# Product with edge_w: three of seven products of each column group split again into seven of half size, their operand sums on GpSimd, the stage written in a fixed order

## The chip, the cores and the metric

The kernel runs on one core of a Trainium2 chip. The metric is the device time of one execution in microseconds. Before the change it is 1904.14 us, the median of three runs (1903.38 to 1904.72). In this text TensorE is PE in the profile, VectorE is DVE, ScalarE is ACT, GpSimd is POOL and SyncE, which issues most loads, is SP.

## The reference, cut to what matters

Inputs are x (4096 x 512), adj (4096 x 4096, about 1.6% of it positive, the rest zero), and the weights of two graph layers. Everything is float32.

```python
x = layernorm(x + relu(adj @ (max(sign(x), 0) @ sign(w0).T)))     # layer 0
node_att = softmax(x @ node_w, axis=0)                            # layer 1, on the new x
h = x @ edge_w                                                    # 4096 x 512: the stage of the change
e = where(adj > 0, h @ h.T, -9e15)
out = adj * (node_att * softmax(e, axis=1)) @ (x @ w1)
x = layernorm(x + out + bias)
```

## The kernel before, in words

**Stages.** The core computes layer 0 row block by row block (up to 505 us), then h (505 to 602 us), then the products h @ h.T with their masked exponentials (602 to about 1000 us), and then the aggregation. This change is in the second stage, and in how it meets the first and the third.

**The product with edge_w.** The new x lies transposed in SBUF as x1T, four slabs of 128 features by 4096 nodes. Wanted is h transposed, hT, of the same shape. The 4096 nodes are eight column chunks of 512; chunk g and chunk g + 4 form column group g (g = 0 to 3). edge_w is cut into 2 x 2 blocks of 256 x 256, and x1T of one group into 2 x 2 blocks of 256 x 512. The function seven (L90) multiplies these 2 x 2 blocks with seven products instead of eight, in the manner of Strassen and Winograd. The seven left operands (left_h) are l11, l12, s4, l22, s1, s2, s3, with four sums made once per kernel by GpSimd (L480 to L483). The right operands are r11, r21, r22, t4, t1, t2, t3, with four differences (t1 to t4) per group made by VectorE in rights_h (L498 to L504) one group ahead. A product is number m = 0 to 6: left operand m times right operand m. It has two halves q (128 rows of output each, one PSUM bank each), and each half takes two matmuls of 128 x 128 by 128 x 512. So a group is 28 matmuls 512 columns wide. A float32 matmul shows as two weight loads and two matmul instructions in the trace.

**Sums of products.** Six PSUM banks (three pairs) hold the running sums. When a product ends, ScalarE copies a bank to hT (L113, L127), or VectorE adds a bank to a block of hT (L116, L122, L123, L131, L135): ten additions of 128 x 512 and four copies per group. c11, c12, c21, c22 are the four blocks of hT of the group; c21 and c22 are the lower feature half, c12 and c22 the chunk g + 4. Tiles of PSUM and SBUF come from pools with a fixed number of buffers, and a new tile waits until an earlier one is no longer read. Accesses of different engines to one PSUM bank are put in sequence, also where they touch different columns.

**What runs beside it.** After each half of a product, between_h is called. It steps the last row block's leftovers from layer 0 (late: eight small VectorE sums, L394 to L397, and DMA issues from GpSimd, L399 and L400), the next group's differences, and premask (L331 on). premask turns pieces of adj (128 x 1024) into bf16 masks: SyncE loads a piece into a buffer (L345, 512 KB), VectorE turns it into a mask in place (L339), GpSimd issues the store to DRAM (L340, 256 KB), and the buffer is loaded again. 26 of 80 pieces are left for this stage. Seven buffers go round (pieces of the tiles more, single, ends and sums_l), and a piece is masked when only three buffers are free, so a load has several calls of time to land. The next stage reads the masks back.

**Order.** Tile's scheduler sets the order of the instructions on each engine in this stage, from dependencies and its own estimate of times; VectorE and ScalarE (not TensorE) are in a written order in the stage before. The last row block of layer 0 ends inside this stage: its normalisation (L356 to L363) on VectorE and its transposes (L419) on TensorE. The next stage begins with operand sums for its own products on VectorE (L783 to L796, L874 to L877, L892 to L895, L908 to L921), which need the finished hT and memory that this stage gives up.

Of the kernel before, what the change touches and what calls it, by code (L numbers as in the profile page):

```python
# [11 lines left out]
F32 = mybir.dt.float32  # L12
# [17 lines left out]
def kernel(  # L30
# [59 lines left out]
    def seven(lop, rop, dests, after):  # L90

# [6 lines left out]
        def multiply(bank, m, first, then):  # L98
            for q in range(2):
                for k in range(K):  # L100
                    nc.tensor.matmul(  # L101
                        banks[bank][q],
                        lop(m, q)[k],
                        rop(m)[k],
                        start=(first and k == 0),
                        stop=(k == K - 1),
                        skip_group_check=not first,
                    )
                then(banks[bank][q], q, *dests[q])
                after(None, None)  # L110

        def m1(ps, q, c11, c12, c21, c22):
            nc.scalar.copy(c21, ps)  # L113

        def u2(ps, q, c11, c12, c21, c22):
            nc.vector.tensor_add(c12, c21, ps)  # L116
# [28 lines left out]

# [13 lines left out]
    with (  # L159
# [270 lines left out]
        with tc.manual_schedule(engines={mybir.EngineType.DVE, mybir.EngineType.Activation}):  # L430
            for n in range(NB):
# [62 lines left out]
        def rights_h(g):  # L494
# [1459 lines left out]
```

## Time and profile before

| | |
|---|---|
| median of three runs | 1904.14 us |
| profiled execution, its own time | 1903.96 us |
| its span | 1902.2 us |
| TensorE busy, of the span | 1890.8 us (99%) |
| VectorE, ScalarE, GpSimd busy | 1527.5, 1024.6, 314.1 us |
| product with edge_w, first to last matmul | 505.2 to 602.1 us |
| matmul instructions of L101 | 224 (two per matmul) |

A line of a timeline reads: start, duration, engine, line of the kernel, operation, output <- inputs, shapes, and how many instructions are merged. In the table of stages each engine has its busy time and the number of its instructions, then the granted TensorE clock, the share of the DMA engines that was busy, and GB/s. "Landing" is the time from the issue of a DMA to its completion.

### The profile page before, as it was taken

The numbers are of one execution on the slowest core, as the hardware profiler recorded it, in microseconds if no ns is written. First come the engines' busy times: TensorE is split into PE (matmuls) and PEld (weight loads), VectorE is DVE, ScalarE is ACT, GpSimd is POOL, SyncE is SP. The second block draws the span as 40 slices with busy tenths as digits, with TensorE's granted clock in tenths as the row PEclk, the third lists the DMA queues.
The fourth block names the chain that finished last, engine by engine and source line by source line (L and its number), as shares of the span: only waits on it lengthen the run. The fifth ranks groups of instructions, "written<-read, shape, count | busy, mean of one in ns | idle before, by whom it ended". The sixth has DMA issues, their size and how long they took to land.

```text
span 1902.2 us, 21262 instructions
## 1 busy us (share of the span) xinstructions
PE 1890.8 (99%) x7054; PEld 1263.4 (66%) x7054; DVE 1527.5 (80%) x2421; ACT 1024.6 (54%) x1669; POOL 314.1 (17%) x449
## 2 busy tenths in 40 slices
PE   9999999999999999999999999999999999999998
PEld 6888888888645656565667556666666666656646
DVE  7777677776877689888896887898879988898947
ACT  6433333333211567666777666665676567667732
POOL 0133132232331111111110111111111101110100
PEclk9999999999999999999999999999999999999999
DMA  9889898898585379577795978878777878787831
GB/s 321 299 322 362 308 339 323 330 353 321 179 295 190 141 267 346 191 259 277 286 334 166 327 279 297 287 288 300 273 278 287 294 270 277 268 318 253 286 114 56
DMA packets 143919, 521.00 MB, mean 274 GB/s; under 512 B 15040, under 2 KB 15040, under 8 KB 136128
## 3 DMA queue, kind: packets, MB, share of 16 engines
q1 hardware_dynamic: 64368, 235.43, 36.7%
q0 software_dynamic: 67632, 248.54, 34.2%
q10 hardware_dynamic: 11808, 35.66, 5.0%
q8 instruction: 56, 0.92, 0.2%
q14 instruction: 55, 0.45, 0.1%
HBM read 397.93 MB, written 121.63 MB: 273 GB/s over the span
## 4 chain that ended last, share of the span: by engine, by line
PE 89%; DVE 7%; ACT 2%; DMA 1%; issue 1%; ACTq 0%; SPq 0%; DVEq 0%
PE bank L1413 33%; PE acc L460 11%; PE acc L459 11%; PE bank L1011 11%; PE seven L101 5%; PE po L1563 4%; PE pt L707 3%; PE bank L806 2%; PE bank L970 2%; PE bank L933 2%; PE bank L745 2%; DVE lent L1182 1%; PE pt L419 1%; DVE slot L1182 1%; PE acc L253 1%
## 5 line engine op out<-in xcount | busy, mean ns | idle before, releaser
L1413 PE MATMUL bank<-lent,lop 128*128 128x256 f32 (+1 forms) x1368 | 433.0, 466 | 1.1 <-DVE lent L1194 0.7
L459 PE MATMUL acc<-xw,hi 128*128 128x512 f32 x960 | 376.4, 392 | 0.0
L460 PE MATMUL acc<-xw,lo 128*128 128x512 f32 x960 | 374.2, 390 | 0.0
L1413 PEld LDWEIGHTS bank<-lent,lop 128*128 128x128 f32 x1368 | 259.3, 190 | 146.1 <-issue 119.9
L1413 PE MATMUL bank<-slot,lop 128*128 128x512 f32 (+1 forms) x928 | 335.4, 508 | 0.4 <-DMA lop<-lop_d 0.2
L1413 PEld LDWEIGHTS bank<-slot,lop 128*128 128x128 f32 x928 | 176.0, 190 | 136.8 <-issue 121.3
L449 ACT CAST hi<-at 128x1024 fp32r<-128x1024 f32 x120 | 126.5, 1054 | 203.2 <-PE acc L459 152.9
L1424 ACT COPY over<-bank 128x512 f32<-128x512 f32 x200 | 116.0, 585 | 198.1 <-PE bank L1413 194.5
L460 PEld LDWEIGHTS acc<-xw,lo 128*128 128x128 f32 x960 | 180.3, 188 | 37.1 <-DVE lo L451 0.3
L459 PEld LDWEIGHTS acc<-xw,hi 128*128 128x128 f32 x960 | 180.3, 188 | 36.8
L451 DVE TENSOR_TENSOR lo<-at,hi 128x1024 fp32r<-128x1024 f32 x120 | 147.8, 1232 | 64.6 <-ACT hi L449 64.1
L678 ACT ACTIVATE line<-line,nmax_c 128x512 f32<-128x512 f32 x160 | 115.2, 726 | 22.4 <-DVE nmax_c L669 22.0
L669 DVE CUSTOM_DVE_ANT_0 line<-lent,slot 128x512 f32<-128x512 bf16 x144 | 93.1, 687 | 9.5 <-ACT slot L708 6.8
L1575 DVE SCALAR_TENSOR_TENSOR xb<-po,f,xb 128x256 f32<-128x256 f32 x84 | 40.3, 481 | 75.0 <-PE po L1563 70.8
L1386 ACT COPY bank<-over 128x512 f32<-128x512 f32 x144 | 86.8, 603 | 0.0
L707 PEld LDWEIGHTS pt<-ident,lent 128*128 128x128 f32 x406 | 50.9, 141 | 36.6 <-issue 24.2
L745 PE MATMUL bank<-hT 128*128 128x512 f32 (+3 forms) x256 | 75.1, 433 | 0.0
L1182 DVE CUSTOM_DVE_ANT_1 lent<-lent,line 128x2048 f32<-128x2048 f32 x32 | 73.0, 2283 | 1.1 <-DMA lent<-s_d 1.1
L708 ACT COPY slot<-pt 128x512 f32<-128x512 f32 (+3 forms) x125 | 68.0, 554 | 10.8 <-PE pt L707 10.8
L420 ACT COPY x1T<-pt 128x512 f32<-128x512 f32 x32 | 18.8, 587 | 101.7 <-PE pt L419 101.7
L1188 ACT ACTIVATE slot<-slot 128x2048 f32<-128x2048 f32 x35 | 67.3, 1924 | 10.8 <-DMA slot<-in_adj_t_dram 10.8
L1182 DVE CUSTOM_DVE_ANT_1 slot<-slot,line 128x2048 f32<-128x2048 f32 x32 | 73.1, 2284 | 0.0
(356 smaller groups left out, 3280.1 us busy)
## 6 DMA issues: line engine op xcount, KB each, us to landing
lop<-lop_d SPq DMA_DIRECT2D x154, 512.0 KB, 4.4
at<-in_adj_t_dram SPq DMA_DIRECT2D x60, 1024.0 KB, 7.3
slot<-in_adj_t_dram POOLq DMA_DIRECT2D x37, 1024.0 KB, 8.1
s_d<-slot POOLq DMA_DIRECT2D x32, 1024.0 KB, 7.6
slot<-s_d POOLq DMA_DIRECT2D x31, 1024.0 KB, 7.4
lent<-s_d POOLq DMA_DIRECT2D x29, 1024.0 KB, 8.2
lent<-in_adj_t_dram POOLq DMA_DIRECT2D x27, 1024.0 KB, 7.6
lent<-in_adj_dram SPq DMA_DIRECT2D x48, 512.0 KB, 6.2
```

Source lines behind the costliest of these rows:

```text
L101: nc.tensor.matmul(banks[bank][q], lop(m, q)[k], rop(m)[k], start=(first and k == 0), stop=(k == K - 1), skip_group_check=not first,)
L449: nc.scalar.copy(hi, aq)
L451: nc.vector.tensor_sub(lo, aq, hi.bitcast(F32))
L459: nc.tensor.matmul(acc, hi[:, c, :], xw[:, kb, :], start=(kb == 0), stop=False)
L460: nc.tensor.matmul(acc, lo[:, c, :], xw[:, kb, :], start=False, stop=(kb == NB - 1))
L678: nc.scalar.activation(line, line, AF.Exp, bias=nmax_c[:, b, c : c + 1], scale=-1.0, accum_out=sum_c[:, b, c : c + 1])
L707: nc.tensor.transpose(pt[:, j, :], src[:, ts(j, P)], ident)
L745: nc.tensor.matmul(pe[:, lo * P :], hT[:, k, ts(A * BG + i, P)], hT[:, k, (B * BG + lo) * P : (B + 1) * W], start=(k == 0), stop=(k == KD ...
L1011: nc.tensor.matmul(ps, left[m][:, k, q, :], right[m][:, k, :], start=(first and k == 0), stop=(k == KD // 2 - 1), skip_group_check=not first,)
L1182: pinned[0](nc.vector._custom_dve(TENSOR_ADD_SAT, out=q, in0=q, in1=m, s0=0.0, s1=-HUGE))
L1413: nc.tensor.matmul(ps, lop[:, k, :], rop[:, k, :], start=start, stop=(k == K - 1), skip_group_check=True)
L1424: nc.scalar.copy(self.to(), self.bank[:, : self.w])
```

## The change

Three of the seven products of a group (m = 0, 4 and 5; in the first group only m = 5) are cut once more into 2 x 2 blocks: left 128 x 128, right 128 x 256. Such a product becomes seven matmuls 256 columns wide (quarters) instead of four matmuls 512 wide. The inner operand sums, four left ones of 128 x 128 once per split product (inner_left) and four right ones of 128 x 256 per split product and group (inner_right), are made by GpSimd. Inside quarters, y is one half of a PSUM tile of its own in which matmuls 0, 5 and 6 are summed; ScalarE copies the running sum after each of them into the quarters x11, x12, x21 and x22 of the product's two banks; z, matmul 4, is copied to SBUF (zs) and added to x12 and x22 by VectorE; matmuls 1, 2 and 3 are accumulated on top.

The order of the products within a group becomes 0 and 4 (interleaved, with the second half of the previous group's product 3 between), then 5 interleaved with 1, then 2, 6 and the first half of 3. For VectorE, ScalarE and TensorE the whole stage is in the written order (manual_schedule). between_h is called twelve times per group and names the call (n of 12) at which each difference t1 to t4 (make) and each set of inner sums (inside) of the next group is made. Masks are now made in 27 calls after the twelfth, three of every four. Their buffers are the four halves of the two more tiles, and sums_l from the sixteenth call on; single and ends are used for inner sums instead. A piece is masked when only one buffer is free.

```diff
@@ -87,61 +87,110 @@
     xw = big.tile([P, NB, D], F32R, name="xw", tag="large")
-    def seven(lop, rop, dests, after):
+    def seven(lop, rop, dests, after, inner, spare, over):
         K = len(rop(0))
         banks = [[ps_mm.tile([P, W], F32, name="seven", tag="mm") for q in range(2)] for _ in range(3)]
...
+        def product(bank, m, first, then):
             for q in range(2):
+                ps = banks[bank][q]
                 for k in range(K):
                     nc.tensor.matmul(
...
+                        ps, lop(m, q)[k], rop(m)[k], start=(first and k == 0), stop=(k == K - 1), skip_group_check=not first
                     )
-                then(banks[bank][q], q, *dests[q])
-                after(None, None)
-        def m1(ps, q, c11, c12, c21, c22):
-            nc.scalar.copy(c21, ps)
-        def u2(ps, q, c11, c12, c21, c22):
-            nc.vector.tensor_add(c12, c21, ps)
+                    if k == K - 1:
+                        then(ps, *dests[q])
+                    yield
+        def quarters(bank, m, z):
+            left, right = inner[m]
+            own = ps_tr.tile([P, W], F32, name="own", tag="tr")
+            y = own[:, :HD]
+            alone_ = z is None
+            z = own[:, HD:] if alone_ else z
+            (x11, x12), (x21, x22) = ((x[:, :HD], x[:, HD:]) for x in banks[bank])
+            zs = spare()
+            def multiply(ps, n, first=False):
+                nc.tensor.matmul(ps, left[n], right[n], start=first, stop=True, skip_group_check=True)
+            multiply(y, 0, True)
+            if not alone_:
+                nc.scalar.copy(x11, y)
+            yield
+            multiply(z, 4, not alone_ and bank == 0)
+            if alone_:
+                nc.scalar.copy(x11, y)
+            yield
+            multiply(y, 5)
+            nc.scalar.copy(x12, y)
+            nc.scalar.copy(zs, z)
+            yield
+            multiply(y, 6)
+            nc.scalar.copy(x22, y)
+            nc.scalar.copy(x21, y)
+            yield
+            multiply(x11, 1)
+            yield
+            multiply(x12, 2)
+            nc.vector.tensor_add(x12, x12, zs)
+            yield
+            multiply(x21, 3)
+            nc.vector.tensor_add(x22, x22, zs)
+            yield
...
-        def u3(ps, q, c11, c12, c21, c22):
-            nc.vector.tensor_add(c22, c21, ps)
-            nc.vector.tensor_add(c22, c22, banks[2][q])
-            after(q, 3)
-        def m2(ps, q, c11, c12, c21, c22):
+        def mix(order, *gens):
...
+            for n, k in enumerate(order):
+                next(gens[k])
+                if n % 4 == 3:
+                    after()
...
+            if len(order) % 4 > 1:
+                after()
+        def alone(gen):
+            for n, _ in enumerate(gen):
+                if n % 2:
+                    after()
+        def m1(ps, c11, c12, c21, c22):
             nc.scalar.copy(c11, ps)
-            after(q, 0)
-        def m4(ps, q, c11, c12, c21, c22):
+        def m6(ps, c11, c12, c21, c22):
+            nc.vector.tensor_add(c22, c22, ps)
+        def m3(ps, c11, c12, c21, c22):
             nc.vector.tensor_add(c21, c21, ps)
-            after(q, 2)
-        def m3(ps, q, c11, c12, c21, c22):
+        def m2(ps, c11, c12, c21, c22):
             nc.vector.tensor_add(c12, c12, ps)
-            after(q, 1)
-        multiply(0, 0, True, m1)
-        multiply(1, 5, True, u2)
-        multiply(2, 4, True, nothing)
-        multiply(1, 6, False, u3)
-        multiply(0, 1, False, m2)
-        multiply(1, 3, False, m4)
-        multiply(2, 2, False, m3)
+        if 0 in inner:
+            z = [banks[1][0][:, h * HD : (h + 1) * HD] for h in range(2)]
+            order = (0, 1, 0, 1, 2, 0, 1, 2, 0, 1, 0, 1, 0, 1, 0, 1)
+            mix(order, quarters(0, 0, z[0]), quarters(2, 4, z[1]), over[0])
+        else:
+            alone(product(0, 0, True, nothing))
+            alone(product(2, 4, True, nothing))
+        for q, (c11, c12, c21, c22) in enumerate(dests):
+            nc.scalar.copy(c21, banks[0][q])
+        for q, (c11, c12, c21, c22) in enumerate(dests):
+            nc.vector.tensor_add(c22, c21, banks[2][q])
+        mix((0, 0, 1, 0, 1, 1, 0, 0, 0, 1, 0), quarters(1, 5, None), product(0, 1, False, m1))
+        for q, (c11, c12, c21, c22) in enumerate(dests):
+            nc.vector.tensor_add(c12, c21, banks[1][q])
+        alone(product(2, 2, False, m2))
+        alone(product(1, 6, False, m6))
+        over[0] = product(1, 3, False, m3)
+        next(over[0])
+        next(over[0])
+        after()
...
                     bufs.clear()
-                    bufs.extend((single, ends))
                     we_s = wp.tile([P, KD, D], F32, name="we_s")
                     nc.sync.dma_start(we_s, edge_w.rearrange("(k p) o -> p k o", p=P))
...
+        def inner_left(L, to):
+            l11, l21, l12, l22 = (L[:, k, ts(f, P)] for k in range(2) for f in range(2))
+            s1, s2, s3, s4 = (to[:, n, :] for n in range(4))
+            tc.keep_in_program_order(nc.gpsimd.tensor_add(s1, l21, l22))
+            nc.gpsimd.tensor_sub(s2, s1, l11)
+            nc.gpsimd.tensor_sub(s3, l11, l21)
+            tc.keep_in_program_order(nc.gpsimd.tensor_sub(s4, l12, s2))
+            return l11, l12, s4, l22, s1, s2, s3
+        def inner_right(R, *to):
+            r11, r12, r21, r22 = (R[:, k, ts(c, HD)] for k in range(2) for c in range(2))
+            t1, t2, t3, t4 = to
+            nc.gpsimd.tensor_sub(t1, r12, r11)
+            nc.gpsimd.tensor_sub(t2, r22, t1)
+            nc.gpsimd.tensor_sub(t4, r21, t2)
+            nc.gpsimd.tensor_sub(t3, r22, r12)
+            return r11, r21, r22, t4, t1, t2, t3
+        def sixteenth():
+            return [x[:, ts(n, HD)] for x in (rows.tile([P, D], F32, name="right_i", tag="rows") for _ in range(2)) for n in range(2)]
+        ends_i = wp.tile([P, 4, HD], F32, name="ends_i", tag="ends")
+        to_i = {0: [ends_i[:, n, :] for n in range(4)]}
+        left_b = wp.tile([P, 4, P], F32, name="left_b", tag="quarter", bufs=2)
+        lefts_i = {5: inner_left(s2, left_b)}
+        inners = [{} for _ in range(HG)]
         more = [stream.tile([P, 2, 2 * W], F32, name="more", tag="stream") for _ in range(2)]
         bufs.extend(m[:, n, :] for m in more for n in range(2))
-        bufs.append(sums_l.rearrange("p n f -> p (n f)"))
-        for _ in range(4):
-            premask(nc.sync, 0, 3)
+        for _ in range(3):
+            premask(nc.sync, 0, 1)
         count = [0]
-        rights = {}
...
-            count[0] += q is None
...
+        over = [None]
+        class Rights:
+            def __init__(self, g):
+                self.r11, self.r12 = (x1T[:, :HK, ts(c, W)] for c in (g, g + HG))
+                self.r21, self.r22 = (x1T[:, HK:, ts(c, W)] for c in (g, g + HG))
+                self.t = {}
+            def make(self, n):
+                tag = "hi" if n < 3 else "lo"
+                t = self.t[n] = sp.tile([P, HK, W], F32, name="t12" if n < 3 else "t34", tag=tag)
+                a, b = {
+                    1: (self.r12, self.r11),
+                    2: (self.r22, self.t.get(1)),
+                    3: (self.r22, self.r12),
+                    4: (self.r21, self.t.get(2)),
+                }[n]
+                nc.vector.tensor_sub(t, a, b)
+            def of(self, m):
+                return (self.r11, self.r21, self.r22)[m] if m < 3 else self.t[4 if m == 3 else m - 3]
+        rights = [Rights(g) for g in range(HG)]
+        for n in (1, 2, 3, 4):
+            rights[0].make(n)
+        to_i[5] = sixteenth()
+        inners[0][5] = lefts_i[5], inner_right(rights[0].t[2], *to_i[5])
+        to_i[4] = sixteenth()
+        zs_ = deque((wp.tile([P, HD], F32, name="z_s", tag="scr"), wp.tile([P, HD], F32, name="z_s", tag="warm")))
+        def inside(g, m, R):
+            inners[g][m] = lefts_i[m], inner_right(R, *to_i[m])
+        def between_h():
+            count[0] += 1
+            g, n = divmod(count[0], 12)
+            if count[0] > 6:
                 next(late[-1], None)
...
+            if count[0] == 16:
+                assert next(late[-1], None) is None
+                bufs.append(sums_l.rearrange("p n f -> p (n f)"))
+            if count[0] == 7:
+                for m, x, tag in ((0, l11, "nw_b"), (4, s1, "bias_b")):
+                    to = wp.tile([P, 4, P], F32, name="left_i", tag=tag)
+                    lefts_i[m] = inner_left(x, to)
+            if g + 1 < HG:
+                if n == 4:
+                    rights[g + 1].make(1)
+                if n == 4 + 4 * (not g):
+                    inside(g + 1, 0, rights[g + 1].r11)
+                    inside(g + 1, 4, rights[g + 1].t[1])
+                elif n == 7:
+                    rights[g + 1].make(2)
+                    inside(g + 1, 5, rights[g + 1].t[2])
+                elif n == 11:
+                    rights[g + 1].make(3)
+            if n == 2 and 0 < g:
+                rights[g].make(4)
+            if count[0] > 12 and count[0] % 4:
+                premask(nc.sync, 0, 1)
+        with tc.manual_schedule(engines={mybir.EngineType.DVE, mybir.EngineType.Activation, mybir.EngineType.PE}):
+            for g in range(HG):
+                right_h = rights[g]
+                seven(
+                    lambda m, q: [left_h[m][:, k, ts(q, P)] for k in range(HK)],
+                    lambda m, r=right_h: [r.of(m)[:, k, :] for k in range(HK)],
+                    [[hT[:, q + f, ts(c, W)] for f in (0, HK) for c in (g, g + HG)] for q in range(2)],
+                    between_h,
+                    inners[g],
+                    lambda: zs_.rotate() or zs_[0],
+                    over,
+                )
+            for _ in over[0]:
+                pass
         assert not loaded and not pieces
```

More of the change, by code (lines that the diff above doesn't have):

```diff
@@ L88 @@
     xw = big.tile([P, NB, D], F32R, name="xw", tag="large")
-    def seven(lop, rop, dests, after):
+    def seven(lop, rop, dests, after, inner, spare, over):
         K = len(rop(0))
         banks = [[ps_mm.tile([P, W], F32, name="seven", tag="mm") for q in range(2)] for _ in range(3)]
-        def multiply(bank, m, first, then):
+        def product(bank, m, first, then):
             for q in range(2):
+                ps = banks[bank][q]
                 for k in range(K):
                     nc.tensor.matmul(
[L102 to L107, printed above, removed]
-                    )
-                then(banks[bank][q], q, *dests[q])
-                after(None, None)
-        def m1(ps, q, c11, c12, c21, c22):
-            nc.scalar.copy(c21, ps)
-        def u2(ps, q, c11, c12, c21, c22):
-            nc.vector.tensor_add(c12, c21, ps)
+                        ps, lop(m, q)[k], rop(m)[k], start=(first and k == 0), stop=(k == K - 1), skip_group_check=not first
+                    )
+                    if k == K - 1:
[35 more added lines that the diff above has]
+            yield
@@ L118, in nothing @@
         def nothing(*_):
             pass
-        def u3(ps, q, c11, c12, c21, c22):
-            nc.vector.tensor_add(c22, c21, ps)
-            nc.vector.tensor_add(c22, c22, banks[2][q])
-            after(q, 3)
-        def m2(ps, q, c11, c12, c21, c22):
+        def mix(order, *gens):
+            gens = [list_ for list_ in gens]
+            for n, k in enumerate(order):
+                next(gens[k])
+                if n % 4 == 3:
+                    after()
+            for gen in gens:
+                assert next(gen, None) is None
+            if len(order) % 4 > 1:
+                after()
@@ L489 @@
-        for _ in range(4):
-            premask(nc.sync, 0, 3)
+        for _ in range(3):
+            premask(nc.sync, 0, 1)
         count = [0]
-        rights = {}
-        def rights_h(g):
-            r11, r12 = (x1T[:, :HK, ts(c, W)] for c in (g, g + HG))
-            r21, r22 = (x1T[:, HK:, ts(c, W)] for c in (g, g + HG))
-            t1, t2 = (sp.tile([P, HK, W], F32, name="t12", tag="hi") for _ in range(2))
-            nc.vector.tensor_sub(t1, r12, r11)
-            nc.vector.tensor_sub(t2, r22, t1)
-            yield
-            t3, t4 = (sp.tile([P, HK, W], F32, name="t34", tag="lo") for _ in range(2))
-            nc.vector.tensor_sub(t3, r22, r12)
-            yield
-            nc.vector.tensor_sub(t4, r21, t2)
-            rights[g] = r11, r21, r22, t4, t1, t2, t3
-            yield
@@ L508 @@
-        ahead_h = deque(p for g in range(1, HG) for p in [rights_h(g)] * 3)
-        for _ in rights_h(0):
-            pass
-        def between_h(q, n):
-            count[0] += q is None
-            if q is None and count[0] > 1:
-                next(late[-1], None)
-            if q is None and count[0] % 14 in (8, 10, 13) and ahead_h:
-                next(ahead_h.popleft())
-            if q is None and count[0] > 6 and count[0] % 5 % 2 == 0:
-                premask(nc.sync, 0, 3)
-        for g in range(HG):
-            right_h = rights.pop(g)
-            seven(
-                lambda m, q: [left_h[m][:, k, ts(q, P)] for k in range(HK)],
-                lambda m: [right_h[m][:, k, :] for k in range(HK)],
-                [[hT[:, q + f, ts(c, W)] for f in (0, HK) for c in (g, g + HG)] for q in range(2)],
-                between_h,
-            )
+        over = [None]
```

## The prediction

> **What bounds the kernel now.** I read the page first, for the bound. TensorE is busy 99% of the span at the full granted clock.
>
> ```profile
> span 1902.2 us, 21262 instructions
> PE 1890.8 (99%) x7054; PEld 1263.4 (66%) x7054; DVE 1527.5 (80%) x2421; ACT 1024.6 (54%) x1669; POOL 314.1 (17%) x449
> PEclk9999999999999999999999999999999999999999
> ```
>
> Then the table of stages, cut at the borders of the four column groups of the product with edge_w.
>
> ```profile
> core 0: us, PE busy (x) PEld busy (x) DVE busy (x) ACT busy (x) POOL busy (x), PEclk, DMA share, GB/s
> 505.20:529.99 24.79, 24.68 (x62) 10.97 (x61) 21.96 (x43) 5.50 (x10) 10.61 (x15) 1.00 0.42 137
> 529.99:554.03 24.04, 24.04 (x58) 10.64 (x57) 16.86 (x24) 2.34 (x4) 5.80 (x8) 1.00 0.93 337
> 554.03:578.07 24.04, 24.04 (x58) 10.65 (x57) 16.19 (x23) 2.34 (x4) 6.53 (x9) 1.00 0.84 277
> 578.07:602.09 24.02, 24.02 (x57) 10.63 (x56) 13.75 (x21) 2.34 (x4) 4.18 (x7) 1.00 0.19 67
> ```
>
> TensorE pauses for 0.1 of these 96.9 us, so a matmul less is time less and each new pause is time more. VectorE is 57 to 89% busy, ScalarE nearly idle, and the mask transfers keep the DMA engines 93% busy in the second group.
>
> The chain and the timeline of TensorE price a matmul (two instructions each).
>
> ```profile
> 510.41 88.42 PE seven L101 x206
> ```
>
> ```profile
> 675.40 0.59 PE L970 MATMUL bank<-hT,lent 128*128 128x256 f32 x2
> 675.83 0.59 PE L1011 MATMUL bank<-right,left 128*128 128x512 f32 x1
> ```
>
> 88.42/206 is 0.429 us an instruction, 0.86 a matmul 512 wide; one 256 wide gives way to the next after 0.43.
>
> The timelines of VectorE and GpSimd show what GpSimd's combinations do to VectorE.
>
> ```profile
> 484.43 0.42 DVE L407 TENSOR_TENSOR sums_l<-xb 128x256 f32<-128x256 f32 x1
> 484.76 1.51 DVE L408 TENSOR_TENSOR sums_l<-xb 128x256 f32<-128x256 f32 x1
> 486.30 1.41 DVE L409 TENSOR_TENSOR sums_l<-sums_l,xb 128x256 f32<-128x256 f32 x1
> 487.75 1.39 DVE L410 TENSOR_TENSOR sums_l<-xb,sums_l 128x256 f32<-128x256 f32 x1
> ```
>
> ```profile
> 484.60 1.38 POOL L480 TENSOR_TENSOR lops<-we_s 128x512 f32<-128x512 f32 x1 [2.20 <-DVE lo L451]
> 485.95 1.48 POOL L482 TENSOR_TENSOR lops<-we_s 128x512 f32<-128x512 f32 x1
> 487.39 1.47 POOL L481 TENSOR_TENSOR lops<-lops,we_s 128x512 f32<-128x512 f32 x1
> 491.44 1.30 POOL L483 TENSOR_TENSOR lops<-we_s,lops 128x512 f32<-128x512 f32 x1
> ```
>
> L407 takes 0.42 us; L408 to L410, of the same form, take 1.4 to 1.5, each ending 0.3 us after a GpSimd instruction ends. They take turns.
>
> **The change part by part**, against the profiled execution: span 1902.2, with what lies around it 1903.96 us, 0.2 under the median 1904.14.
>
> *Removed: matmul time.* A product of four matmuls 512 wide (3.44 us) becomes seven 256 wide (3.01). Ten products are split (one, then three times three): 10 x 0.43 = 4.3 us off TensorE's path. This is also the most that can be gained.
>
> *Added on ScalarE:* five PSUM copies of 256 columns per split, 50 x 0.37 us (L833) = 18.5 us, beside TensorE, on an engine that is busy 2.3 of 24 us per group. In the written order a copy has at least 0.86 us of other matmuls before its reader: nothing, unless ScalarE itself waits for a late VectorE addition.
>
> *Added on VectorE:* two additions of 256 columns per split, 20 x 0.34 (L838 takes 0.41, back to back 0.34) = 6.8 us. The 512-wide additions stay ten per group. Hidden by VectorE's spare 7 us per group, so long as nothing is held up in its queue.
>
> *Added on GpSimd:* 40 combinations of 128x256 and 12 of 128x128. Scaling L483's 1.30 us for 512, I take 0.66 and 0.33 (bounds: 0.5 to 0.75, since L480 to L482 took up to 1.48), 30 us in all; GpSimd has 27 of 97 us filled. Its time is hidden; its effect on VectorE and the lateness of its results are not. [...]
>
> *Moved: waits.* Five places can give the gain back.
>
> (a) First group into second. GpSimd gets, from the seventh step on (13.3 us into the group: 12 matmuls of 0.86 and 7 of 0.43), 8 x 0.33 + 9 x 0.66 = 8.6 us before the combination that the second inner product reads, and three DMA issues of the last row block (0.75 each, as L399 and L400): 13.3 + 8.6 + 2.3 = 24.2 us. TensorE is there at 21.9 + 3 x 0.43 = 23.2: 1.0 us. In the same stretch VectorE has 6.3 us of work (1.13 + four 0.6 + eight small L394 to L397 at 0.2 to 0.34 + 0.6) before product 3 may overwrite its bank 6.9 us later, and nine of its operations read two SBUF tensors and can be held 0.66 each: 0 to 5, I take 0.6, since half are held only after the addition that matters.
>
> (b) Groups two and three, product 6. It waits for the first c12 addition, behind a right-hand sum (1.13), a mask (0.6) and an inner addition (0.34): with 0.6 for itself and 0.34 for signals, 3.0 us against 3.44 for the four matmuls between. One hold of 0.66 exceeds that by 0.2, two by 0.9; GpSimd is working then. 0.5 each, 1.0 together (0 to 2).
>
> (c) Masks. Queries by line give the landing times, loads (L345) first, stores (L340) second:
>
> ```profile
> DMA to landing us min/median/max: 3.9/5.2/8.0
> ```
>
> ```profile
> DMA to landing us min/median/max: 2.5/5.4/6.3
> ```
>
> A buffer is masked (0.6), stored, loaded and masked again. At the medians that is 11.5 us, at the minima 7.3. Before, seven buffers go round, about 20 us each; after, five, reused after five of nine steps per 22.8 us group: 12.7 us on average, 11.2 in the shortest stretch. A store behind a run of eight combinations in GpSimd's queue starts 2 to 3 us later. VectorE's queue then stops at the mask, and the additions behind it make TensorE wait beyond 0.5 to 1 us of slack. I expect two or three such stops of 1 to 2 us, 1.5 us on TensorE (0 to 6).
>
> (d) Into the next stage. VectorE's chain from L874 (599.46) to L911 (612.45) is on the path there. The last masks now lie just ahead of it, and L874, L875 (1.13 each) may slip behind the end: 0 to 2.3, I take 0.8.
>
> (e) Last row block. TensorE took its transposes 0.1 us after L362 had ended. GpSimd's first four combinations run at that time and can hold L504 ahead of it: 0.3 (0 to 1.3).
>
> Weighed in (a) and (b): additions with one operand in PSUM (L116 to L135) are counted as not held, since no row shows one beside a GpSimd sum. [...]
>
> Sum: -4.3 + 1.0 + 0.6 + 1.0 + 1.5 + 0.8 + 0.3 = +0.9: 1903.96 + 0.9, rounded 1905 us.
>
> **The rivals.**
>
> *The order hides everything.* Only 0.3 us of (a) to (e) is left: 1904.0 - 4.0 = 1900 us. For it: the matmuls between copy and reader cover each ScalarE copy. Against: GpSimd's turns with VectorE in the rows above, which cost up to 1 us each. Halfway, 1902.
>
> *The mask buffers become the bound (slower).* If the round trip is 13.7 us instead of 11.5 it exceeds the 12.7 that five steps give, by 1.0 per round; 27 steps make 5.4 rounds per buffer and so 5.4 us on VectorE's queue, all of it TensorE's once the slack is gone, in place of (c)'s 1.5: 1905 + 3.9 = 1909 us. For it: ten loads waited 24.4 us in all for stores (SP's waits) even with seven buffers; 337 GB/s in the second group. Against: no VectorE mask waited for a load then. It decides once store plus load exceed 12 us.
>
> *GpSimd is slower than scaled.* At 0.75 and 0.4 us, 52 combinations take 4.4 us more, in just the runs that TensorE or VectorE wait for: 1908 us.
>
> *No gain in the matmuls.* A 256-wide instruction lasts 0.215 us against 0.19 for its weight load (PEld of L970). If each of the 70 inner matmuls shows one load, 70 x 0.19 = 13 us: 1918. L970 runs at 0.43 among others, so this is remote.
>
> **How the numbers follow.** A measurement of this kernel tells about 0.2%, 3.8 us, from no change: faster means under 1900.3, slower over 1907.9. Chances: forecast (1902 to 1908) 0.42; everything hidden, or halfway to the forecast, 0.28, of which 0.2 below 1900.3; masks 0.17; GpSimd 0.12; no gain 0.01. So 0.2 faster. Slower: masks and GpSimd, 0.29, the remote 0.01 and 0.06 of the forecast's upper edge, 0.36. Same: 0.44. The range runs from 1900, the hidden case, to 1911, above both slow rivals; less than 2 in 10 is outside. Within the likeliest case it is 1902 to 1908.
>
> **What would show it.** Matmuls of the split products in 256-wide groups at 0.43 us; a stage of about 97 us in all, as long as the 96.9 before; TensorE waits named after GpSimd's right_i tiles or VectorE's hT additions at the start of the second group and at product 6; VectorE rows L339 waiting for DMA; make sums at 1.5 to 2 us beside GpSimd. I am wrong if those waits are absent (hidden), if L339 waits add up to over 4 us (masks), or if the time is lost behind the stage.

## The result, and the profile after

The change makes the kernel slower: 1923.7 us (median of four runs, 1922.79 to 1925.46) against 1904.4 us (1903.38 to 1904.94), a ratio of 1.0103 with a 95% interval from 1.0086 to 1.0121. The forecast was 1905 us with a range up to 1911.

The page of the kernel after, profiled in a run of 1924.15 us:

```profile
span 1922.4 us, 21567 instructions
PE 1892.9 (98%) x7114; PEld 1277.3 (66%) x7114; DVE 1543.1 (80%) x2441; ACT 1041.2 (54%) x1719; POOL 359.1 (19%) x501
PEclk9999999999999999999999999999999999999999
```

TensorE's busy time grew by 2 us and the span by 20: the time is mostly in pauses. The stage table, cut as before at the first matmul of each column group (the first column is the stretch and its length, then the busy time of each engine with its number of instructions, the granted TensorE clock, the DMA share and GB/s):

```profile
504.58:529.24 24.66, 22.80 (x64) 11.26 (x63) 18.90 (x36) 7.11 (x15) 13.86 (x20) 1.00 0.20 70
529.24:559.13 29.89, 25.05 (x75) 14.71 (x74) 20.57 (x30) 7.33 (x19) 13.29 (x19) 0.94 0.38 123
559.13:594.95 35.82, 25.89 (x75) 14.99 (x74) 21.61 (x31) 7.33 (x19) 27.07 (x33) 0.86 0.70 234
594.95:620.68 25.73, 25.12 (x79) 14.50 (x78) 18.79 (x33) 7.26 (x19) 8.22 (x10) 1.00 0.80 268
```

The stage takes 116.1 us instead of 96.9, 19.2 us more, and holds nearly all of the 20.2 by which the span grew; what comes before and behind it changed by -0.6 and +1.6 us. Groups two and three lose most, and in them alone the granted clock is below 1. The view of TensorE's waits in the stage (total, times, longest) says what it stood for; before, it named none here:

```profile
PE seven L99 <- ACT hT L182: 11.6, 2, 9.9
PE own L116 <- POOL right_i L547: 3.2, 1, 3.2
PE seven L99 <- DVE hT L166: 1.2, 1, 1.2
PE pt L468 <- DVE xb L411: 0.7, 1, 0.7
PE seven L99 <- DVE hT L187: 0.6, 1, 0.6
```

One pause of 9.92 us is over half of it. It ends on ScalarE's c21 copy, but ScalarE had been waiting for VectorE's inner addition, and VectorE for a mask load. The timelines of TensorE, ScalarE and VectorE, each with its idle time and what ended it in brackets:

```profile
578.12 2.07 PE L99 MATMUL seven<-x1T,we_s 128*128 128x512 f32 x2 [9.92 <-ACT hT L182]
```

```profile
577.48 1.24 ACT L182 COPY hT<-seven 128x512 f32<-128x512 f32 x2 [11.72 <-DVE seven L137]
```

```profile
568.77 0.92 DVE L388 TENSOR_SCALAR more<-more 128x1024 bf16<-128x1024 f32 x1 [6.49 <-DMA more<-in_adj_dram]
...
574.49 0.87 DVE L388 TENSOR_SCALAR more<-more 128x1024 bf16<-128x1024 f32 x1 [3.06 <-DMA more<-in_adj_dram]
576.41 0.69 DVE L388 TENSOR_SCALAR more<-more 128x1024 bf16<-128x1024 f32 x1 [1.06 <-DMA more<-in_adj_dram]
577.02 0.76 DVE L137 TENSOR_TENSOR seven<-seven,z_s 128x256 f32<-128x256 f32 x2
```

A mask load waits until the store of the mask that was in its buffer has landed, and the stores are issued by GpSimd. The longest wait of SyncE's queue for such a store was 12.1 us (the last number of the line), against 6.5 us before:

```profile
SPq L394 <- DMA mask_d<-more: 60.5, 18, 12.1
```

The mask made at 547.34 is stored at 562.22, and only then can the load start for which VectorE waits 6.49 us at 568.77. GpSimd's timeline shows why the stores were late:

```profile
518.98 0.73 POOL L546 TENSOR_TENSOR right_i<-t 128x256 f32<-128x256 f32 x1
525.34 0.38 POOL L650 PARTITION_ALL_REDUCE gmax<-nmax  x1 [5.63 <-issue]
532.79 0.71 POOL L546 TENSOR_TENSOR right_i<-t 128x256 f32<-128x256 f32 x1 [7.07 <-PE own L116]
...
541.78 0.82 POOL L547 TENSOR_TENSOR ends_i<-x1T,ends_i 128x256 f32<-128x256 f32 x1
548.57 0.40 POOL L656 PARTITION_ALL_REDUCE gsum<-nsum  x1 [5.97 <-PE own L116]
548.86 1.65 POOL L389 DMA_DIRECT2D mask_d<-more  x2
557.56 0.71 POOL L548 TENSOR_TENSOR ends_i<-x1T,ends_i 128x256 f32<-128x256 f32 x1 [7.05 <-issue]
...
562.22 0.90 POOL L389 DMA_DIRECT2D mask_d<-more  x1
...
566.67 0.73 POOL L389 DMA_DIRECT2D mask_d<-more  x1 [0.75 <-PE seven L116]
```

L650 and L656 are the two all-reduces of the node softmax, written behind the stage. Tile's scheduler puts them into the middle of it, since their inputs are ready early. An all-reduce itself takes 0.4 us, but GpSimd stands still for 5.6 and 6.0 us ahead of the two, and for 7.1 us ahead of the first combination behind each: 25.7 us in four stops. Two of them are named after TensorE's `own`, but that event had long passed; they are as long as the ones named "issue". Each of the four begins with a GpSimd instruction that stands nowhere else in this stage (a line of this view: the kernel's line, the instruction, its number, its shortest, median and longest ns, its first and last start):

```profile
L650 POOLq MODIFY_POOL_CONFIG  x2: 12/14/16, 519.7 to 519.7; - x2
L546 POOLq MODIFY_POOL_CONFIG  x2: 83/83/83, 525.7 to 525.7; - x2
L656 POOLq MODIFY_POOL_CONFIG  x2: 109/109/109, 542.7 to 542.7; - x2
L548 POOLq MODIFY_POOL_CONFIG  x2: 42/42/42, 550.6 to 550.6; - x2
```

So there is one stop with this instruction for each all-reduce, and one for the way back to combinations; what GpSimd does in a stop, no row shows.

The kernel before has the same two all-reduces in the same stage, with one such instruction, under the first (L536, at 515.8): nothing between them or behind them was a combination, and there is no stop for a way back. Its one stop, of 6.21 us, is in its trace:

```profile
521.78 0.38 POOL L536 PARTITION_ALL_REDUCE gmax<-nmax  x1 [6.21 <-issue]
...
527.34 0.76 POOL L542 PARTITION_ALL_REDUCE gsum<-nsum  x1 [0.20 <-ACT node_att L540]
```

My reading was therefore: (A) the four stops make inner sums and mask stores late, and that is the loss. The rivals were (B) five mask buffers are too few by themselves, and (C) GpSimd and VectorE hinder each other at every operation (masks took 0.9 to 1.3 us beside sums, instead of 0.69).

### The profile page after: what moved, and what is told of

Same layout as the page of the kernel before. It is cut to its first block, busy times and chain, and to the rows that moved or that the text cites. A ratio compares the mean times of both kernels' runs of the same rounds, so it can differ in the third digit from the quotient of the medians.

```text
span 1922.4 us, 21567 instructions
## 1 busy us (share of the span) xinstructions
PE 1892.9 (98%) x7114; PEld 1277.3 (66%) x7114; DVE 1543.1 (80%) x2441; ACT 1041.2 (54%) x1719; POOL 359.1 (19%) x501
## 5 line engine op out<-in xcount | busy, mean ns | idle before, releaser
L822 ACT COPY slot<-pt 128x512 f32<-128x512 f32 (+3 forms) x125 | 68.1, 554 | 11.5 <-PE pt L821 11.5
L1302 ACT ACTIVATE slot<-slot 128x2048 f32<-128x2048 f32 x35 | 67.3, 1923 | 10.4 <-DMA slot<-in_adj_t_dram 10.3
```

## The experiments

In all of them "stage" is the time from the first matmul of the product with edge_w to the first of the next stage, and pauses are those of TensorE inside it.

### Both all-reduces behind the stage, in either kernel

The kernel after (and, as a control, the kernel before, whose lines differ):

```diff
-    nc.gpsimd.partition_all_reduce(gmax, nmax, P, bass_isa.ReduceOp.max)
+    tc.keep_in_program_order(nc.gpsimd.partition_all_reduce(gmax, nmax, P, bass_isa.ReduceOp.max))
...
-    nc.gpsimd.partition_all_reduce(gsum, nsum, P, bass_isa.ReduceOp.add)
+    tc.keep_in_program_order(nc.gpsimd.partition_all_reduce(gsum, nsum, P, bass_isa.ReduceOp.add))
```

> The kernel after, with both all-reduces of the node softmax held in written order, so that GpSimd does them behind the product with edge_w and no longer between its combinations and mask stores. Theory A (GpSimd's four stops of 6 to 7 us around the two all-reduces cause the loss): the pauses of 1.16, 3.17, 1.67 and 9.92 us on TensorE and the 1.7 + 2.7 us of lower clock behind them go, 20.3 us in all; 1923.7 - 20.3 = 1903.4, taken as 1902 to 1908; the stage takes 96 to 100 us instead of 116, VectorE waits under 4 us for mask loads. Rival B (five mask buffers are too few): the first stop (3.17 + 1.74) goes, but VectorE goes on waiting some 15 us for mask loads and TensorE most of 9.9 us for that: 1915 to 1920. Rival C (GpSimd and VectorE hinder each other, sums and masks at 0.9 to 1.3 us instead of 0.6 to 0.7): nothing of that depends on the all-reduces, 1918 to 1924.

> The control: the kernel before with the same two all-reduces held behind the stage. Theory A: before, nothing behind the all-reduces was late for TensorE, so moving them changes nothing: 1904.4, within 1 us, stage 97 us. If moving them is worth something by itself (they delayed mask stores there too) it is faster, 1900 to 1903; if the first panels then wait for the all-reduce that now comes at the stage's end, 1906 to 1910, and the same would be in the kernel after with both moved.

Measured, kernel after: 1904.58 us, ratio to the kernel before 1.0000 (0.9992 to 1.0009). The 19 us are gone. Stage table and TensorE's waits:

```profile
504.93:528.16 23.23, 22.53 (x64) 11.32 (x63) 19.42 (x34) 5.41 (x12) 20.19 (x27) 1.00 0.22 75
528.16:551.54 23.38, 23.15 (x76) 13.89 (x75) 20.58 (x30) 7.26 (x19) 16.08 (x21) 1.00 0.62 214
551.54:575.14 23.60, 23.38 (x76) 14.06 (x75) 20.46 (x30) 7.26 (x19) 16.88 (x21) 1.00 0.83 272
575.14:601.09 25.95, 24.75 (x79) 14.49 (x79) 19.26 (x33) 7.26 (x19) 7.52 (x10) 1.00 0.83 294
```

```profile
PE seven L99 <- ACT hT L182: 1.6, 3, 1.2
PE pt L468 <- DVE xb L411: 0.7, 1, 0.7
```

The stage takes 96.16 us, VectorE waits 3.5 us for mask loads instead of 15.0, and no wait for right_i is left. GpSimd's timeline has one stop where it had four:

```profile
606.31 2.08 POOL L650 PARTITION_ALL_REDUCE gmax<-nmax  x1 [6.14 <-ACT slot L869]
608.26 0.38 POOL L674 MEMSET nmax_c<- 128x256 f32 x1
608.52 0.38 POOL L675 MEMSET sum_c<- 128x256 f32 x1
609.61 0.68 POOL L656 PARTITION_ALL_REDUCE gsum<-nsum  x1 [0.72 <-ACT node_att L654]
```

With memsets between the two all-reduces GpSimd is idle for 0.72 us ahead of the second, with combinations between them it stood for 7.07 and 5.97 us. The control, the kernel before with the same edit, takes 1902.97 us, ratio 0.9993 (0.9984 to 1.0002), with a stage of 96.88 us and no pause: there the stop cost nothing that can be measured. A holds; B and C, which left 11 us or more, fall as causes of the loss.

The two profiled runs are not typical: that of the kernel after is the fastest of its eleven (1902.47 us), that of the control the slowest of its eleven (1904.88 us). By the medians, taken on the same chip, the kernel after is 1.6 us slower than the control, although the stage in its trace is 0.7 us shorter; no trace shows where the rest goes.

### One all-reduce behind the stage

The exponential between the two all-reduces is held in written order, which takes the second with it; the first stays ahead of the second group's inner sums.

```diff
-    nc.scalar.activation(node_att, node_s, AF.Exp, bias=gmax, accum_out=nsum)
+    tc.keep_in_program_order(nc.scalar.activation(node_att, node_s, AF.Exp, bias=gmax, accum_out=nsum))
```

> The kernel after with the exponential of the node softmax held in written order on ScalarE: the second all-reduce (the sum) goes behind the stage, the first (the maximum) stays where it was, ahead of the second group's inner sums. Theory A: of the four stops two are left. The pauses of 1.16 and 3.17 us and 1.74 us of lower clock stay, 6.1 us; those of 1.67 and 9.92 us with 2.7 us of lower clock, 14.2 us, go: 1923.7 - 14.2 = 1909.5, taken as 1907 to 1912. Rival B (mask buffers): the long pause of the third group stays in the main, 1917 to 1923. Rival C: 1920 to 1924.

Measured: 1913.43 us, ratio 1.0044 (1.0031 to 1.0057), so by the medians 10 us of the 19 are gone with the second pair of stops and 9 go with the first. The profiled run itself took 1909.37 us, as expected, with a stage of 102.03 us: by the traces the split is 14.1 and 5.9 us. The other four, from 1912.8 to 1914.85, are longer by 3.4 to 5.5 us. Their mean granted clock is 0.997 or 0.998 against 0.999, which can be part of it; no trace shows the rest, so the split is open. The pauses of the first pair stand as they were, and the long one of the third group is gone:

```profile
528.22 1.98 PE L99 MATMUL seven<-t,we_s 128*128 128x512 f32 x4 [1.32 <-DVE hT L166]
...
536.32 0.70 PE L116 MATMUL own<-right_i,left_i 128*128 128x256 f32 x2 [3.10 <-POOL right_i L547]
...
567.24 1.12 PE L99 MATMUL seven<-x1T,we_s 128*128 128x512 f32 x2 [0.22 <-ACT hT L182]
```

### Five mask buffers in the kernel before

```diff
-                    bufs.extend((single, ends))
...
-            premask(nc.sync, 0, 3)
+            premask(nc.sync, 0, 1)
```

(the second edit at both calls)

> The kernel before with five mask buffers in the product with edge_w instead of seven (each masked with one left free instead of three, as in the kernel after); no splits. Theory A: five buffers go round in 14 us at three steps in five of 1.72 us, against a round trip of 11.5 us at the medians of load and store, so they suffice: 1904.4 to 1907, VectorE waits under 4 us for mask loads. Rival B: the buffers are the bound: VectorE waits 10 us or more for mask loads and TensorE pauses for it, 1908 to 1918.

Measured: 1904.85 us, ratio 1.0004 (0.9995 to 1.0013), stage 96.88 us, no pause. Five buffers alone cost TensorE nothing in that kernel. They are not free for VectorE: it waited 10.4 us for mask loads (7.0 and 3.4 us by tile, the longest 2.4), where theory A had under 4, but none of it reached TensorE.

### Mask stores on another queue

By which of GpSimd's two kinds of work did the second pair of stops reach TensorE? All-reduces as in the kernel after, the stage's mask stores issued by SyncE:

```diff
-                nc.gpsimd.dma_start(mask_d[r][:, c : c + 2, j, :], m)
+                (nc.sync if count[0] else nc.gpsimd).dma_start(mask_d[r][:, c : c + 2, j, :], m)
```

> The kernel after, all-reduces where they were, but the mask stores of the stage issued from SyncE's queue instead of GpSimd's. It tells by which of GpSimd's two kinds of work the second pair of stops reaches TensorE. Theory A1 (the mask stores: late stores, late loads, VectorE stopped at a mask, additions behind it): the pause of 9.92 us with 0.35 us of lost overlap and 2.7 us of lower clock goes although GpSimd still stops four times for 6 to 7 us; the pause of 3.17 us for right_i stays: 1923.7 - 12.9 = 1910.8, taken as 1908 to 1914. Theory A2 (the late inner sums): both stay, 1920 to 1925. If SyncE's queue, which then holds loads behind stores that wait for masks, becomes the bound instead: VectorE waits over 5 us for mask loads, 1912 to 1920.

Measured: 1917.8 us, ratio 1.0070 (1.0057 to 1.0084), stage 108.66 us. GpSimd still stops (6.76 and 7.45 us ahead of combinations), and the 9.92 us are now 2.66; the pause for right_i stays:

```profile
535.20 1.22 PE L116 MATMUL own<-right_i,left_i 128*128 128x256 f32 x2 [2.87 <-POOL right_i L547]
...
570.32 1.12 PE L99 MATMUL seven<-x1T,we_s 128*128 128x512 f32 x2 [2.66 <-ACT hT L182]
595.53 1.35 PE L99 MATMUL seven<-x1T,we_s 128*128 128x512 f32 x2 [2.00 <-ACT hT L182]
```

So the late stores carried at least 7.3 of the 9.92 us, as A1 said. The time is above A1's 1908 to 1914 and in the third case's range: SyncE's queue now holds loads behind stores that wait for masks, VectorE still waits 8.7 us for mask loads, and a pause of 2.00 us is new.

### What a pause costs beside itself

In the kernel after TensorE's clock is not full behind the long pauses (0.50 in windows behind those of 3.17 and 9.92 us). Two kernels were to make pauses in the kernel before (both all-reduces behind the stage) by repeating a ScalarE copy of the bank that the next group needs:

```diff
-            nc.scalar.copy(c11, ps)
+            for _ in range(1 + q * extra):
+                nc.scalar.copy(c11, ps)
```

> What a pause of TensorE costs beside itself: the kernel before with both all-reduces behind the stage, and ScalarE made to copy the same PSUM bank 18, 20 and 24 times more in groups 1, 2 and 3, so that the next group's first matmuls into that bank wait some 2, 3.5 and 6 us. Theory A (a pause of 3 us or more is followed by some 3.5 us at half the granted clock, a shorter one by none; each loses some 0.35 us of overlap): the granted clock stays 1.00 behind the first and falls to 0.5 behind the second and third; the stage grows by the sum of the pauses, 1 us of overlap and 3.5 to 5.5 us of lower clock. Rival (the lower clock in the kernel after had to do with its other work, not with the pauses): the clock stays 1.00 and the stage grows by the pauses and 1 us alone.

> The pauses again, with longer chains: 26, 29 and 34 extra copies instead of 18, 20 and 24. In the run before, a copy took 0.615 us and 15.45 us of them were hidden, so that only the 24 stopped TensorE, for 0.77 us; by that the pauses are now 2.0, 3.8 and 6.9 us, 12.7 in all. Theory A (a pause of about 3 us or more is followed by some 3.5 us at half the granted clock): 1.00 behind the first, 0.5 to 0.8 behind the second and third; stage 96.9 + 12.7 + 1.0 of overlap + 3.5 to 5.5 = 114 to 116 us. Rival (the clock has to do with other work): 1.00 throughout, 110.6 us.

Both missed their aim. ScalarE's order is not written there, the scheduler spread the copies, and the pauses came out at 0.77 us in the first, and 0.29, 0.43 and 0.94 us in the second (single runs of 1904.37 and 1905.89 us). They price short pauses: the stages, of 97.91 and 99.33 us, are 1.03 and 2.45 us above 96.88, that is the pauses and 0.26 us for each. The clock stayed at 1.00. In the kernel after, ScalarE's order is written, so the chain went there, with both all-reduces behind the stage; `extra` is 0, 4, 7 and 11 in groups 1 to 4:

```diff
         for q, (c11, c12, c21, c22) in enumerate(dests):
-            nc.scalar.copy(c21, banks[0][q])
+            for _ in range(1 + extra * (1 - q)):
+                nc.scalar.copy(c21, banks[0][q])
```

> What a pause of TensorE costs beside itself, this time with chains whose place is sure: the kernel after with both all-reduces behind the stage, and ScalarE (whose order is written there) makes the first c21 copy 4, 7 and 11 times more in groups 2, 3 and 4, just where TensorE already waited 0.23, 0.22 and 1.20 us for it. At 0.615 us a copy the pauses are 2.7, 4.5 and 8.0 us, 13.5 us more than without. Theory A (a pause of about 3 us or more is followed by some 3 to 4 us at about half the granted clock): clock 0.5 to 0.8 behind the second and third, perhaps the first; the stage takes 96.2 + 13.5 + 3.5 to 6 us of lower clock, 113 to 116 us. Rival (the lower clock in the kernel after had another cause than the pauses): 1.00 throughout, 109.7 us.

Measured (one run): 1924.58 us, stage 114.21 us; the pauses are 2.70, 4.54 and 6.56 us. Windows around the first (the clock is the third number from the right):

```profile
536.70:539.40 2.70, 0.02 (x1) 0.00 (x0) 2.24 (x3) 2.57 (x6) 1.51 (x3) 1.00 0.66 247
539.40:541.40 2.00, 1.97 (x4) 1.15 (x5) 1.99 (x3) 0.74 (x2) 1.92 (x4) 0.66 0.58 174
541.40:543.40 2.00, 2.00 (x4) 0.88 (x4) 0.26 (x1) 0.65 (x2) 1.52 (x2) 0.50 0.85 336
543.40:545.40 2.00, 2.00 (x9) 1.39 (x8) 0.00 (x0) 1.09 (x3) 0.00 (x0) 0.99 0.40 145
```

Behind the second, which ends at 568.73, three windows of 2 us have 0.50, 0.50 and 0.64. Against the stage of 96.16 us with 1.65 us of these waits, the pauses account for 12.15 us; the other 5.9 us are the clock behind three pauses, about 2 us each. The lower clock comes from pauses alone, without late masks or sums.

Length alone does not decide it: in the kernel with the stores on SyncE, a pause of 2.66 us left the clock at 1.00 and one of 2.00 us did not. The record of the clock in the traces says more. Inside the kernel the granted clock changes only on a grid of 3.41 us, and it stays low for one, two or three steps of it (in the kernel after from 535.52 to 538.93 and from 573.07 to 583.31, one step and three, with ten between them). Cut on this grid, the pause of 2.66 us (567.66 to 570.32) is split over two steps, and that of 2.00 us (593.53 to 595.53) lies in one:

```profile
565.57:568.98 3.41, 2.09 (x10) 1.51 (x8) 1.80 (x2) 0.00 (x0) 3.33 (x5) 1.00 0.91 291
568.98:572.39 3.41, 2.07 (x6) 1.08 (x7) 3.41 (x8) 1.78 (x5) 1.45 (x2) 1.00 0.90 305
592.88:596.29 3.41, 1.41 (x5) 0.51 (x4) 2.47 (x6) 1.33 (x3) 0.00 (x0) 1.00 0.85 247
596.29:599.71 3.42, 3.42 (x6) 1.85 (x6) 1.91 (x4) 0.99 (x4) 0.00 (x0) 0.50 0.73 242
```

TensorE is idle for 39% of each of the first two steps and for 59% of the third; only the third is followed by 0.50. In all thirteen traces, from the first whole step on, every step at full clock with 59% or more idle was followed by a step at 0.50 (15 of them, some at the end of the kernel), and of those with up to 50% idle only one was (48%, in the control, 8 us after its start). In the kernel after the steps from 532.11 and 569.65, idle for 91% and 100%, are followed by 0.50, those from 542.35 and 566.24, idle for 49% and 43%, by 1.00. No run varied this on purpose.

### Can VectorE's order keep the 4.3 us?

With the all-reduces moved, 2.35 us of pauses were left, 1.65 us of it for c21 copies. Just ahead of the additions that these copies need (L137, L140), VectorE has a whole right-hand sum and two masks; ahead of the copy that TensorE waited for longest (1.20 us) the second mask had also waited 1.34 us for its load. Three orders were tried, all with both all-reduces behind the stage. First, the fourth right-hand sum, the second one and the mask of step 3 moved to later steps:

```diff
-            if n == 2 and 0 < g:
+            if n == 4 and 0 < g:
                 rights[g].make(4)
...
-                elif n == 7:
+                elif n == 9:
                     rights[g + 1].make(2)
...
-            if count[0] > 12 and count[0] % 4:
+            if count[0] > 12 and n not in (0, 3, 4):
                 premask(nc.sync, 0, 1)
```

> The kernel after with both all-reduces behind the stage and VectorE's written order changed so that no mask and no whole right-hand sum lies directly ahead of the inner additions of products 0 and 4 (the fourth right-hand sum two steps later, the second two steps later, the mask of step 3 gone, one at step 8 instead). With the all-reduces alone moved, TensorE waited 0.23, 0.22 and 1.20 us for the c21 copies that stand behind those additions, each wait with some 0.35 us of lost overlap: 2.7 us of the 4.3 saved. Theory A: these go, the stage takes 93.5 us instead of 96.2, 2.7 us under the run with the all-reduces alone moved (1904.6): 1901 to 1903. Rival: VectorE's work is only moved, and the additions that then come late (c22 ahead of product 2, c12 ahead of product 6) stop TensorE as much: 1903 to 1907.

Measured: 1906.46 us, ratio 1.0010 (1.0001 to 1.0019), stage 96.89 us. Two c21 waits went, but the moved right-hand sum held up the additions of product 6 (0.26 and 1.61 us), and late masks cost 0.89 and 1.63 us in the next stage (VectorE's L897 there waited 1.77 us for the transfer of a mask). One addition (L445) took 2.63 us instead of 0.42 beside GpSimd's sums:

```profile
528.47 2.63 DVE L445 TENSOR_TENSOR low<-sums_l,low 128x256 f32<-128x256 f32 x1
```

Second, with these two moves taken back where they hurt:

```diff
-                elif n == 9:
+                elif n == (9 if g else 7):
...
-            if count[0] > 12 and n not in (0, 3, 4):
+            if count[0] > 12 and n not in ((0, 3, 8) if g > 2 else (0, 3, 4)):
```

> Both all-reduces behind the stage, and the new order of VectorE kept only where it paid: in the first group the second right-hand sum is back at step 7 (its place at step 9 held up the additions of product 6: 0.26 and 1.61 us of waits), in the last group the mask of step 3 goes to step 4, just behind the inner additions, instead of step 8 (the late masks there cost 0.89 and 1.63 us in the next stage). Theory A: of the waits for c21 copies (0.23, 0.22, 1.20 us with the all-reduces alone moved) the first two go and the third is halved, nothing comes back, 1.5 to 2.5 us under the run with the all-reduces alone moved: a stage of 94 us, 1901 to 1903. Rival: VectorE has no margin left in the stage, and what is taken from one place is missing in the next: stage 96 to 97 us, 1904 to 1906.5.

Measured: 1903.54 us, ratio 0.9991 (0.9982 to 1.0000), stage 95.25 us, but then 1.47 us of waiting in the next stage. Third, two masks moved from the last group into the first:

```diff
+            if n in {0: (5, 6), 3: (1, 2, 4, 5, 6, 7, 9)}.get(g, (1, 2, 5, 6, 7, 8, 9, 10, 11)) and count[0] < 48:
                 premask(nc.sync, 0, 1)
```

> The run with the second new order, and two masks fewer in the last group, two more in the first: at steps 5 and 6, where VectorE waited 2.2 and 0.8 us for inner products. Left in the run before were waits of 1.31 us for c12 additions in the last group (behind a mask that waited for its load) and of 1.47 us in the next stage (VectorE there 1.4 us late behind the last mask). Theory A (in the last group the five buffers are too few for eight masks, and only there): both waits go, with 0.26 us of overlap each 3.3 us: stage 93.9 us, 1900 to 1902. Rival (VectorE or GpSimd have no room in the first group either): the two masks and their stores delay the additions of product 6 or the inner sums of the second group by their own 1.3 and 1.4 us, and it stays at 1903 to 1905.

Measured: 1903.95 us, ratio 0.9998 (0.9989 to 1.0007), stage 96.88 us. The rival held: the last group's wait went, 0.43 us were left in the next stage, and three of 0.64 to 0.81 us for product 6's additions came. In four orders the pauses inside the stage sum to 2.0 to 3.3 us, with those of the next stage to 2.6 (the all-reduces alone moved), 5.8, 3.5 and 3.4 us: they change place or grow. My reading, not tested by itself, is that VectorE, filled 80 of 96 us, has no room left where the other engines wait for it. None beats the kernel before by more than a measurement can tell.

## Why the prediction was wrong

The account of the stage closes in every kernel: -4.3 us of matmuls, the pauses, 0.26 to 0.34 us of lost overlap for each, and the lower clock. For the kernel after: -4.3 + 17.2 + 6 x 0.3 + 4.5 = 19.2 us. The 4.5 is what is left for the clock; the low clock lasts 3.3 us behind the pause of 3.17 us and 5.2 us behind that of 9.92 us, and half of that is 4.3. With both all-reduces moved: -4.3 + 2.35 + 4 x 0.3 = -0.75, measured -0.72.

- *Removed matmul time* was right. Instructions 256 wide follow each other at 0.43 us (528.16, 528.59, 529.02 in the timeline with the all-reduces moved), and no load shows.
- *GpSimd's combinations* were near: 0.72 instead of 0.66 us for 256 columns where nothing disturbs them, 0.44 to 0.72 instead of 0.33 for 128.
- *The failed step* is GpSimd's queue in (a) and (c). In (a) I listed what stands ahead of the second inner product (eight and nine combinations and three issues, 1.0 us late) and left out an instruction that was there before the change: the all-reduce, with 6.21 us of "issue" ahead of it in the trace of before. Worse, I took that queue's cost as the sum of its instructions; the stop on the way back to combinations, which no row of before shows, cost another 7.1 us. The pause was 3.17 us instead of 1.0. That 12.7 us of stops made no longer pause was luck: I had put the first of these combinations at its written place, 13.3 us into the group, and the scheduler put it at 6.1 us (510.64). With the all-reduces moved no wait for right_i is left, so (a)'s own 1.0 us was not there either. The 0.6 us for the c22 addition became 1.16: VectorE's queue held a step of the softmax that waited 2.0 us for the all-reduce (L651), which I had not listed either, and it went with the all-reduces.
- *(c)* had the chain right (store late, load late, VectorE stopped at a mask, additions behind it, TensorE stopped) and the size wrong: "2 to 3 us later" for a store was 10 to 14 us behind the end of its mask (the masks made at 547.34 and 552.22 were stored at 562.22 and 566.67), so 1.5 us, at most 6, became 9.92. With the all-reduces moved it is one pause of 1.20 us, near the 1.5. (The terms of the round trip in the prediction add up to 11.2 and 7.0 us, not 11.5 and 7.3.) The rival of the mask buffers named the right rows, but priced a round trip that is always too long and reaches TensorE in full; with five buffers in the kernel before, VectorE waited 10.4 us for loads and TensorE not at all.
- *The price of a pause* was missing everywhere: waits were added at their length. Lost overlap and clock made 6.3 of the 19.2 us.
- *The turns* of GpSimd and VectorE were real but small: masks took 3.46 us as a pair beside GpSimd's late sums (540.30) instead of 1.28 us, and the 1.67 us pause for c21 follows them. With the all-reduces moved that pause is 0.23 us.
- *(b)* was 0 in the groups it named; its 0.34 us for signals was an estimate of mine (in before, ScalarE's L360 starts at 508.56, 0.04 us after VectorE's L358 has ended, and TensorE's transposes start at 509.75, 0.11 us after L362 has). *(d)* was a wait of 0.25 us instead of 0.8, and *(e)* 0.70 instead of 0.3, both with the all-reduces moved. What I had costed at nothing, the ScalarE copies "unless ScalarE itself waits for a late VectorE addition", was just that case: 0.23, 0.22 and 1.20 us, the last of them by (c)'s late mask.

With the all-reduces moved the time was about as forecast, 1904.58 us against 1905, but that is partly luck. The sum had 5.2 us of waits; the trace has 2.6 ((a) and (b) nothing, (c) 1.20, (d) 0.25, (e) 0.70, two copies 0.45) and some 1.5 us of lost overlap that the sum did not have, and its run, at 1902.47 us, is 2.5 us under the forecast. My test for "masks" (L388 waits over 4 us) fired, at 15.0 us, but the cause stood one queue further back.

## What to carry to other kernels

Before work is put on GpSimd, list everything that its queue holds in that stretch, the scheduler's placements too, and look for idle time named "issue" in front of operations such as the all-reduce: alternating it with plain tensor operations cost 5.5 to 7.5 us here for each change of kind, so keep one kind together. DMA issues behind such a stop wait with it (mask stores came 10 to 14 us behind their masks here), and five buffers without reserve passed it on to VectorE (15.0 us of waits for loads) and TensorE (a pause of 9.92 us), which have no part in the all-reduce's stop. With VectorE busy for 80 of 96 us and others waiting at fixed places of its order, moving its work mostly moved the waits (2.6 to 5.8 us of pauses in four orders); and a pause of the bound engine cost more than its length, by 0.26 to 0.34 us, and by about 2 us more behind those of 2.70, 4.54 and 6.56 us.

## What the runs showed of the hardware that I had not expected

- GpSimd's stop came both ways: 5.5 to 6.7 us ahead of an all-reduce, 6.8 to 7.5 us ahead of the combination that follows one; none between two all-reduces with only DMA issues or memsets between them (0.20 us of idle time in before, 0.72 and 1.71 us with both moved, named after the exponential between the two).
- TensorE's granted clock fell to 0.5 behind pauses of 2.00 to 9.92 us, in steps of 3.41 us: one step for pauses of 2.00, 2.70, 2.87, 3.10 and 3.17 us, two for 4.54 and 6.56, three for 9.92, where the steps of the longer ones began inside the pause. Pauses up to 1.7 us had none, nor had one of 2.66 us that was split over two steps; what went with the fall was a step with TensorE idle for 59% or more.
- A pause, down to 0.22 us, cost 0.26 to 0.34 us beside its length. Rows of TensorE last 0.59 us and begin 0.43 us apart (528.16, 528.59), so by them a restart loses 0.16 us of overlap; where the rest goes is not shown.
